# A two-layer graph attention kernel: fewer pairs in the edge count, and one weight load behind a row

## The chip, the cores and the metric

The kernel runs on one core of one Trainium2 chip. The metric is the device time in microseconds (us) of one launch, as the median of several runs; the kernel before takes 647.35 us (three runs, 647.07 to 647.61). In what follows PE is TensorE (matrix products), DVE is VectorE, ACT is ScalarE, POOL is GpSimd and SP is SyncE, which here only issues DMA transfers. Instructions of one engine start in program order; the engines meet at semaphores.

## The reference

The input is a graph of 512 nodes with 768 features each and 16,896 directed edges: 8,192 random pairs in both directions and 512 self loops, sorted by destination. Two graph attention layers follow each other, the first with 8 heads that are concatenated, the second with one; a residual sum and a layer norm close it.

```python
def gat_layer(x, W, a_s, a_d, b, edge_index, concat):
    h = (x @ W).reshape(n, H, C)
    alpha_s = jnp.einsum('nhc,hc->nh', h, a_s)
    alpha_d = jnp.einsum('nhc,hc->nh', h, a_d)
    e = jax.nn.leaky_relu(alpha_s[src] + alpha_d[dst], NEG_SLOPE)
    m = jax.ops.segment_max(e, dst, num_segments=n)
    e = jnp.exp(e - m[dst])
    denom = jax.ops.segment_sum(e, dst, num_segments=n)
    alpha = e / (denom[dst] + EPS)
    out = jax.ops.segment_sum(h[src] * alpha[:, :, None], dst, num_segments=n)
    ...
h = jax.nn.elu(gat_layer(x, W1, a_src1, a_dst1, b1, edge_index, concat=True))
out = gat_layer(h, W2, a_src2, a_dst2, b2, edge_index, concat=True)
return _layernorm(x + out)
```

Everything is float32.

## The kernel before

**Dense attention.** The kernel works with a 512 x 512 matrix `cnt` that holds how often each (destination, source) edge occurs, and `absent`, a large negative number where it doesn't occur. Per head, a 128-row block of scores is lifted from the row of source logits (`lift`, L465, ACT), bent (`leak`, L471, DVE), lowered to its maximum over the present edges (`rank`, L474, DVE, then an exponential on ACT), weighted with `cnt` and normalised (`weigh`, DVE), and transposed by a DMA (`turn_out` and `turn_in`) into `PT`.

**Products.** All large products are done in seven half-size products, P1 to P7, instead of eight. The sums that this needs of weights are made by loads that add on arrival (issued by POOL, L108 and L119) and by DVE (L303, L304); those of activations by DVE (L291 to L294, L744 to L758). Per head there are three stages: `projection` (x times W1 of the head: 14 products of three matmuls, L311), `mixed` (aggregation over the sources, L783, with the bias and ELU) and `second` (times the 768 rows of W2 that belong to the head, L311, added into `h2`). Each weight slot exists once: head h+2's W1 is loaded into the slots that head h+1's projection has read, and W2 alternates with it in another set.

**Counting the edges.** The first 62 us also make `cnt`. The destinations are sorted, so the 132 chunks of 128 consecutive edges each touch only a narrow span of destination nodes. Chunk c has its centre at m = (c + 0.5) * 128 * 512 / 16896. The kernel cuts the 512 destinations into 16 blocks of 32 and fixes, when it is built, which blocks each chunk may touch: the block of m, and a neighbour if m lies closer than `SLACK` nodes to that neighbour (L228 to L234). Each (chunk, block) is a pair; there are 210, and 78 of the chunks have two. For a pair, a 32-wide one-hot of the destinations (`od`, L509, DVE, a quarter of the chunks at a time, from `rel`, L265, the destination minus the first node of the block) is multiplied with a 512-wide one-hot of the chunk's sources (`os`, L532 on DVE or, for the blocks of the third 128-row block of `cnt`, a step function on ACT, L530). This is a matmul of 128x32 by 128x512 (L558). The result takes 32 rows of a 128-row PSUM bank; the pairs wait in four queues by their place among the four 32-row groups, and `count` (L547) takes one from each queue a round, so that four matmuls in different column groups of the array follow each other.

The order is written out by hand (L578 to L642): nine batches of 16 chunks (the last of 4). For each, DVE makes its one-hots; then a few products of head 0's first projection (`items`) and some DVE extras go out, with ACT making the step functions of the next batch between them; then `count` runs on what is queued. What doesn't fill a round stays queued for the next batch. 32 buffers hold the `os` one-hots; a new one-hot has to wait until the matmuls that read the old one are done.

`below`, `found` and `flag` (L514 to L520, L575) count the pairs whose destination lies in its block. If an edge falls into none of its chunk's blocks the whole pass is done again in a general way (L32); the block rule therefore decides speed, not the result.

**Head 0, and the queues around it.** SP's queue holds, in order: the four DMA transposes of head 0's weights of attention, `load_w2(0)` (L830: one 576 KB and six 384 KB transfers; POOL adds two more on arrival), then in the loop over heads `load_w1(h + 2)` (L854: again seven on SP and two adding ones on POOL), then `row_out` (L454), which is called from inside `mixed`: DVE transposes the source logits (L457), SP writes them in four small transfers to a scratch row in DRAM (L460) and reads them back spread over 128 partitions (L463). Behind it follow the next head's vectors (`load_a`, L868) and four loads for a logit product (`attended`, L841 to L844). `lift(h + 1, 0)` on ACT needs the row. In the loop, the order on DVE is written out too: P1 and P2 of `second` are emptied, the gT sums and two W2 sums are made, and only then `leak` and `rank` of the next head's scores follow.

Of the kernel before, what the change touches and what calls it, by code (L numbers as in the profile page):

```python
# [36 lines left out]
def gat_pass(  # L37
# [18 lines left out]
    N, D = x.shape  # L56
    H = a_src1.shape[0]
# [44 lines left out]
    def load_w(W, h, slot, m):  # L102


        t1 = wpool.tile([P, HK, HALF], F32, name=f"{slot}t1")
        upper = m[:HK * P, :].rearrange("(k p) d -> p k d", p=P)
        nc.sync.dma_start(t1, upper[:, :, L])
        nc.gpsimd.dma_start(t1, upper[:, :, R], accum_op=ALU.add)  # L108
        W[h] = []
        for r in range(2):  # L110
            w = wpool.tile([P, HK, D], F32, name=f"{slot}{r}")
            for k in range(r * HK, (r + 1) * HK):
                nc.sync.dma_start(w[:, k - r * HK, :], m[k * P:(k + 1) * P, :])
            W[h].append(w)
        W[h].append(t1)

        def rest():

            nc.gpsimd.dma_start(W[h][0][:, :, R], m[HK * P:, R].rearrange("(k p) d -> p k d", p=P),  # L119
                                accum_op=ALU.add)  # L120
        return rest

    def load_w1(h, slot="w2"):
        return load_w(W1, h, slot, w1[:, h * D:(h + 1) * D])
# [79 lines left out]
    def turn_x(t, r):  # L204

        ps = mm.tile([P, 512], F32, name="mm")
        for k in range(HK):
            nc.tensor.transpose(ps[:, k * P:(k + 1) * P], x_sb[:, t, (r * HK + k) * P:(r * HK + k + 1) * P], ident)
        nc.scalar.copy(xT[:, r * HK:(r + 1) * HK, t * P:(t + 1) * P],
                       ps[:, :HALF].rearrange("p (k n) -> p k n", n=P))  # L210
# [4 lines left out]
    if general:  # L215
        nc.vector.tensor_copy(idx_f, idx_i)
        idx = ohp.tile([P, 2, EC], F32, name="idx")
        psi = tr.tile([P, 512], F32, name="tr")
        for j in range(2):
            for r in range(2):  # L220
                nc.tensor.transpose(psi[:, (2 * j + r) * EH:(2 * j + r + 1) * EH], idx_f[:, j, r, :],
                                    ident[:EH, :EH])
        nc.vector.tensor_copy(idx, psi[:, :2 * EC].rearrange("p (j c) -> p j c", j=2))
    else:

        B, SLACK = 32, 10  # L228
        blocks = []
        for c in range(EC):  # L230
            m = (c + 0.5) * P * N / E
            b = int(m // B)
            lo, hi = b - (m - b * B < SLACK), b + ((b + 1) * B - m < SLACK)
            blocks.append(range(max(lo, 0), min(hi, N // B - 1) + 1))  # L234
        at = [0]
        for b in blocks:
            at.append(at[-1] + len(b))
        NB = at[EC]
        assert NB + EC <= 512 and max(map(len, blocks)) <= 2


        pick = ohp.tile([EH, NB], F32, name="pick")
        base = ohp.tile([P, NB], F32, name="base")
        lo = 0
        while lo < EC:
            hi, k = lo + 1, len(blocks[lo])
            while hi % EH and blocks[hi] == blocks[lo]:
                hi += 1
            copy = nc.vector.tensor_copy if lo < 5 * EC // 8 else nc.scalar.copy
            copy(pick[:, at[lo]:at[hi]].rearrange("p (c k) -> p c k", k=k),  # L250
                 ident[:EH, lo % EH:(hi - 1) % EH + 1].unsqueeze(2).to_broadcast([EH, hi - lo, k]))
            for j, b in enumerate(blocks[lo]):
                nc.gpsimd.memset(base[:, at[lo]:at[hi]].rearrange("p (c k) -> p c k", k=k)[:, :, j], float(b * B))
            lo = hi
        nc.vector.tensor_copy(idx_f, idx_i)
        turn_x(0, 0)
        psi = tr.tile([P, 512], F32, name="tr")
        for r in range(2):
            cols = slice(at[r * EH], at[(r + 1) * EH])
            nc.tensor.matmul(psi[:, cols], idx_f[:, 0, r, :], pick[:, cols], start=True, stop=True)  # L260
        for r in range(2):
            nc.tensor.transpose(psi[:, NB + r * EH:NB + (r + 1) * EH], idx_f[:, 1, r, :], ident[:EH, :EH])
        turn_x(1, 0)
        rel = ohp.tile([P, NB], F16, name="rel")
        nc.vector.tensor_tensor(rel, psi[:, :NB], base, op=ALU.subtract)  # L265
        idx = ohp.tile([P, EC], F32, name="idx")
        nc.vector.tensor_copy(idx, psi[:, NB:NB + EC])
# [582 lines left out]
                times(R, b1_[:, D:], -1.0, V2)]  # L850

    for h in range(H - 1):
        if h + 2 < H:
            load_w1(h + 2)()  # L854
        else:
            A[H] = []
            for j, a in ((2, a_src2[0]), (4, a_dst2[0])):
                v = wpool.tile([P, HK, HALF], F32, name=f"w2t{j}").rearrange("p k n -> p (k n)")[:, :D]
                nc.sync.dma_start(v, row_bcast(a))
                A[H].append(v)  # L860
            last_sum = load_w2(H - 1, "w2")
        GA, gsums = left(gT, gS)
        halves = [half_logits(h + 1, t) for t in ((0, 1) if h else (0, 1, 3))]
        besides[2:2] = [s_ for s_, _ in halves] + [lambda: row_out(h + 1)]
        finish = mixed(h, AA, BB, besides + [d_ for _, d_ in halves])
        besides = []
        if h + 2 < H:
            load_a(h + 2, a_src1[h + 2], a_dst1[h + 2])  # L868
            attend = attended(h)
        pairs = second(h, GA, B2)  # L870
        for m, _ in pairs[:2]:
            m()
        pairs[0][1]()
        for f in finish:
            f()
        gsums[0]()
        pairs[1][1]()
        gsums[1]()
        if pending:
            pending.pop(0)()  # L880
        pairs[2][0]()
        gsums[2]()
        pairs[3][0]()
        gsums[3]()
        if pending:
            pending.pop(0)()
        pairs[2][1]()
        pairs[3][1]()
        last = h + 2 == H
        q = [lift(h + 1, 0)]  # L890
        for n in range(2, 7):
            (m0, e0), (m1, e1) = pairs[2 * n:2 * n + 2]
            m0()
            if not last:
                m1()
            if n < 6:
                leak(q[n - 2])
                rank(q[n - 2], n - 2)
            if n < 5:
                q.append(lift(h + 1, n - 1))  # L900
            if last:

                if n > 4:
                    turn_in(n - 5)
                if n == 6:
                    turn(q[2], 2)
                if n == 6:
                    weigh(q[3], 3)
                m1(lambda: turn(q[3], 3) if n == 6 else None)
            if not last and n == 6:  # L910
                turn_in(0)
                weigh(q[2], 2)
                turn_out(q[2], 2)
            e0()
            if last and 2 < n < 6:
                weigh(q[n - 3], n - 3)
                if n < 5:
                    turn_out(q[n - 3], n - 3)
            if not last and 3 < n < 6:
                weigh(q[n - 4], n - 4)  # L920
                turn_out(q[n - 4], n - 4)
            if not last and n == 6:
                weigh(q[3], 3)
                turn_out(q[3], 3)
                load_w2(h + 1)()
            e1()
        if h + 2 < H:
            B_, sums = right(W1[h + 2], "w2")
            pairs = projection(h + 2, XA, B_)
            for n in range(14):  # L930
                pairs[n][0]()
                if n == 0:
                    for f in attend:
                        f()
                    B2, sums2 = right(W2[h + 1], "w1")
                if n in (1, 3):
                    sums[n // 2]()
                if n == 1:
                    AA, sums3 = left_sums(h + 1)
                pairs[n][1]()  # L940
                if n in (1, 2, 4):
                    turn_in((n + 2) // 2)
                if n == 5:
                    BB, sums3 = right_sums()
                if 1 <= n < 9:
                    sums3.pop(0)()
                if n in (9, 10):
                    sums2.pop(0)()
                if n in (11, 13):
                    logits(h + 2, HS[h + 2], 2 + (n - 11) // 2)  # L950
        else:
            last_sum()
            B2, sums2 = right(W2[H - 1], "w1")
# [162 lines left out]
```

## Time and profile before

| what | value |
| --- | --- |
| median of three runs | 647.35 us |
| the profiled execution, own time | 647.49 us |
| its span | 645.7 us |
| PE, busy share of the span | 98% |
| DVE | 80% |
| ACT | 44% |
| POOL | 7% |
| mean granted TensorE clock | 0.998 |
| DMA traffic | 100.32 MB, mean 155 GB/s |

The page gives busy time of each engine and the chain of work that ended last. A matmul of 128x384 in float32 shows up as two records of 487 ns that overlap, so a product of three matmuls (six records) takes 2.06 us of PE. Times of the timeline are microseconds from the start of the span; in its lines the figure after the start is how long the group took, the bracket is how long the engine was idle before it and what ended that.

### The profile page before, as it was taken

The page shows a single profiled execution, that of the slowest core. Times are in us where ns is not written, and L with a number is a line of the kernel's source. Part 1 is how long each engine was busy: PE and PEld are TensorE (multiplying, and loading weights), DVE is VectorE, ACT ScalarE, POOL GpSimd, SP SyncE. Part 2 cuts the span into 40 slices and gives each one's busy share as a digit, 9 for nine tenths or more (in the row PEclk, how much of TensorE's full clock was granted, in tenths as well). Part 3 has the DMA queues.
Part 4 walks back from the last instruction along what each step waited for, and adds up shares of the span by engine and source line. Part 5 has one row for each costly group of instructions (what it writes and reads, how often), then busy time and mean ns, then how long its engine had stood idle before and what let it go on. Part 6 is the DMA issues. An engine that isn't in the chain of part 4 may idle for free.

```text
span 645.7 us, 7216 instructions
## 1 busy us (share of the span) xinstructions
PE 634.5 (98%) x2347; PEld 400.6 (62%) x2347; DVE 519.7 (80%) x1149; ACT 281.8 (44%) x484; POOL 46.7 (7%) x90
## 2 busy tenths in 40 slices
PE   8999999999999999999999999999999999999995
PEld 5544585556855586556855586556855586645553
DVE  8999989978789677877789677877789677876885
ACT  6774744530725035430726035430726035543440
POOL 1310020011000110011000110011000110000000
PEclk9999999999999999999999999999999999999999
DMA  9993499296816793196816694196806890410122
GB/s 317 329 208 87 81 334 282 47 262 195 185 48 146 176 257 138 33 259 189 200 36 141 182 257 138 33 261 199 189 36 153 219 257 16 109 47 0 34 57 77
DMA packets 81017, 100.32 MB, mean 155 GB/s; under 512 B 39574, under 2 KB 62926, under 8 KB 80974
## 3 DMA queue, kind: packets, MB, share of 16 engines
q1 hardware_dynamic: 67310, 78.18, 39.2%
q0 software_dynamic: 12976, 20.65, 18.4%
q10 hardware_dynamic: 688, 0.98, 0.5%
q8 instruction: 20, 0.33, 0.2%
q14 instruction: 23, 0.19, 0.1%
HBM read 86.93 MB, written 1.59 MB: 137 GB/s over the span
## 4 chain that ended last, share of the span: by engine, by line
PE 93%; DVE 5%; ACT 0%; issue 0%; DVEq 0%
PE mm L311 62%; PE mm L783 20%; PE mm L729 3%; PE mm L1062 3%; PE held L311 2%; DVE os L532 1%; PE tr L558 1%; PE bc L181 1%; DVE odw L509 1%; DVE scr L320 0%; PE bc L558 0%; PE tr L986 0%; DVE h L367 0%; DVE q L477 0%; DVE q L472 0%
## 5 line engine op out<-in xcount | busy, mean ns | idle before, releaser
L311 PE MATMUL mm<-w,gT 128*128 128x384 f32 x288 | 96.8, 488 | 0.2 <-DVE u L367 0.2
L311 PE MATMUL mm<-w,xT 128*128 128x384 f32 x264 | 88.2, 487 | 0.0
L311 PEld LDWEIGHTS mm<-w,gT 128*128 128x128 f32 x288 | 54.3, 190 | 38.1 <-issue 1.6
L311 PEld LDWEIGHTS mm<-w,xT 128*128 128x128 f32 x264 | 49.9, 190 | 35.5 <-ACT os L530 0.8
L787 ACT COPY u<-mm 128x256 f32<-128x256 f32 x21 | 7.8, 372 | 140.5 <-PE mm L783 140.5
L479 ACT ACTIVATE q<-q,nmax 128x512 f32<-128x512 f32 x36 | 25.8, 721 | 89.5 <-DVE nmax L477 89.5
L783 PE MATMUL mm<-PT,hs 128*128 128x256 f32 x252 | 61.3, 379 | 0.0
L311 PE MATMUL mm<-w1t,gS 128*128 128x384 f32 x180 | 60.6, 486 | 0.0
L311 PE MATMUL mm<-w2t,xS 128*128 128x384 f32 x168 | 56.6, 487 | 0.0
L783 PEld LDWEIGHTS mm<-PT,hs 128*128 128x128 f32 x252 | 47.8, 190 | 8.3 <-issue 0.4
L369 DVE TENSOR_TENSOR h<-h,mm 128x384 f32<-128x384 f32 x72 | 39.1, 550 | 12.5 <-PE mm L311 12.0
L311 PEld LDWEIGHTS mm<-w1t,gS 128*128 128x128 f32 x180 | 34.1, 190 | 24.2 <-issue 0.6
L311 PEld LDWEIGHTS mm<-w2t,xS 128*128 128x128 f32 x168 | 31.8, 190 | 22.4 <-ACT q L468 0.4
L783 PE MATMUL mm<-pS,gS 128*128 128x256 f32 x168 | 43.2, 380 | 0.0
L711 ACT COPY PT<-zr 128x1024 uint16<-128x1024 uint16 x34 | 39.5, 1162 | 2.6 <-DMA zr<-pS 1.9
L783 PEld LDWEIGHTS mm<-pS,gS 128*128 128x128 f32 x168 | 31.8, 190 | 4.7 <-DVE pS L756 0.4
L706 ACT COPY pS<-q 128x1024 uint16<-128x1024 uint16 x26 | 27.2, 1045 | 16.6 <-DVE q L691 16.6
L311 PE MATMUL mm<-w1t,gT 128*128 128x384 f32 x96 | 32.4, 487 | 0.5 <-DVE h L367 0.5
L311 PE MATMUL mm<-w,gS 128*128 128x384 f32 x96 | 32.6, 486 | 0.0
L311 PE MATMUL mm<-w,xS 128*128 128x384 f32 x96 | 32.5, 487 | 0.0
L108 POOL DMA_DIRECT2D w1t<-in_L_gnn_W_dram x7 | 8.9, 1267 | 309.0 <-DVE w2t L304 142.3
L369 DVE TENSOR_TENSOR u<-u,mm 128x384 f32<-128x384 f32 x28 | 15.4, 553 | 18.8 <-PE mm L311 18.7
(190 smaller groups left out, 1083.9 us busy)
## 6 DMA issues: line engine op xcount, KB each, us to landing
w<-in_L_gnn_W_dram SPq DMA_DIRECT2D x90, 384.0 KB
w<-in_L_gnn_W_dram POOLq DMA_DIRECT2D x16, 576.0 KB, 9.0
w2t<-in_L_gnn_W_dram SPq DMA_DIRECT2D x10, 576.0 KB
w1t<-in_L_gnn_W_dram SPq DMA_DIRECT2D x9, 576.0 KB
w2t<-in_L_gnn_W_dram POOLq DMA_DIRECT2D x8, 576.0 KB, 9.2
w1t<-in_L_gnn_W_dram POOLq DMA_DIRECT2D x7, 576.0 KB, 8.7
a_s<-in_L_gnn_a_src_dram SPq DMA_DIRECT2D x8, 384.0 KB
a_d<-in_L_gnn_a_dst_dram SPq DMA_DIRECT2D x8, 384.0 KB
```

The costliest lines, as they stand in the source:

```text
L108: nc.gpsimd.dma_start(t1, upper[:, :, R], accum_op=ALU.add)
L181: nc.tensor.matmul(idle, zeros[:, :P], zeros, start=True, stop=True)
L311: nc.tensor.matmul(ps[:, :HALF], A_[p][:, k, i * P:(i + 1) * P], B_[p][:, k, :], start=start and k == 0, stop=k == HK - 1, skip_group_chec ...
L369: nc.vector.tensor_tensor(a, a, ps, op=ALU.subtract if p == "P7" else ALU.add)
L479: nc.scalar.activation(q, q, AF.Exp, bias=nmax, scale=-1.0)
L509: nc.vector.tensor_tensor(od[:, lo:hi, :], rel[:, lo:hi].unsqueeze(2).to_broadcast([P, hi - lo, B]), nodes[:, :B].unsqueeze(1).to_broadcas ...
L706: nc.scalar.copy(apart.rearrange("p (h n) -> p h n", h=2), q.bitcast(U16).rearrange("p (n h) -> p h n", h=2))
L711: nc.scalar.copy(PT.rearrange("p s n -> p (s n)").bitcast(U16).rearrange("p (s n h) -> p s n h", s=NT, h=2)[:, :, t * P:(t + 1) * P, :], p ...
L729: nc.tensor.matmul(ps[:, :N], HS[h][:, s, c * P:(c + 1) * P], PT[:, s, :], start=(s == 0), stop=(s == NT - 1))
L783: nc.tensor.matmul(bank[p][:, :HN], A_[p][:, k, c * P:(c + 1) * P], B_[p][:, k, :], start=over is None and k == 0, stop=k == 1, skip_group ...
L787: nc.scalar.copy(u, part("P1"))
L1062: nc.tensor.matmul(ps[:, :cols.stop - cols.start], PT[:, s, t * P:(t + 1) * P], h2[:, s, cols], start=(s == 2), stop=(s == 1))
```

## The change

Two things change. The slack that decides which blocks a chunk is paired with is no longer 10 nodes everywhere, but 2 + 16 * sqrt(p * (1 - p)) with p = m / 512, the chunk's place in the sorted list: 3.0 at the ends, 8.9 at a quarter, 10 in the middle. That gives 196 pairs in place of 210, and 64 chunks with two blocks in place of 78. And in head 0 (h = 0 of the loop) `load_w1(2)` is called after `mixed`, hence behind `row_out` on SP, and ahead of `load_a`; in the other heads it stays where it was.

```diff
-        B, SLACK = 32, 10
+        B = 32
         blocks = []
         for c in range(EC):
             m = (c + 0.5) * P * N / E
             b = int(m // B)
-            lo, hi = b - (m - b * B < SLACK), b + ((b + 1) * B - m < SLACK)
+            slack = 2 + 16 * (m / N * (1 - m / N)) ** 0.5
+            lo, hi = b - (m - b * B < slack), b + ((b + 1) * B - m < slack)
             blocks.append(range(max(lo, 0), min(hi, N // B - 1) + 1))
...
     for h in range(H - 1):
-        if h + 2 < H:
+        if 0 < h < H - 2:
             load_w1(h + 2)()
-        else:
+        elif h:
             A[H] = []
...
         finish = mixed(h, AA, BB, besides + [d_ for _, d_ in halves])
         besides = []
+        if h == 0:
+            load_w1(2)()
         if h + 2 < H:
             load_a(h + 2, a_src1[h + 2], a_dst1[h + 2])
             attend = attended(h)
```

## The prediction

> **What bounds the kernel now.** I read the table of busy time first, then the chain that ended last, then busy time by stretch, then the timeline of the two places that the diff touches.
>
> The page and the stretches (cut at the joints of the chain) give the room:
>
> ```profile
> PE 634.5 (98%) x2347; PEld 400.6 (62%) x2347; DVE 519.7 (80%) x1149; ACT 281.8 (44%) x484; POOL 46.7 (7%) x90
> ...
> core 0: us, PE busy (x) PEld busy (x) DVE busy (x) ACT busy (x) POOL busy (x), PEclk, DMA share, GB/s
> 0.00:20.72 20.72, 18.73 (x112) 10.20 (x112) 17.61 (x67) 14.52 (x36) 3.50 (x56) 1.00 0.94 333
> 20.72:41.79 21.07, 20.77 (x122) 10.76 (x122) 19.52 (x50) 14.76 (x28) 5.92 (x5) 1.00 1.09 279
> 41.79:61.80 20.01, 19.14 (x131) 9.47 (x131) 19.10 (x58) 10.99 (x21) 1.78 (x2) 1.00 0.54 116
> 61.80:100.42 38.62, 38.59 (x145) 27.13 (x145) 34.42 (x82) 24.37 (x42) 4.68 (x4) 1.00 0.75 203
> 100.42:117.55 17.13, 16.42 (x50) 8.69 (x48) 16.29 (x29) 5.41 (x10) 0.41 (x1) 1.00 0.82 223
> 117.55:637.50 519.95, 519.92 (x1784) 333.58 (x1785) 410.35 (x859) 210.74 (x350) 30.42 (x24) 1.00 0.54 140
> ```
>
> PE is the bound, and from 117.55 on without a gap. Before that it idles 1.99 + 0.30 + 0.87 + 0.03 + 0.71 us. So a change gains by fewer PE instructions or out of these gaps. The chain shows what closes each gap:
>
> ```profile
> 19.80 0.88 DVE xS L291
> 20.72 6.07 PE mm L311 x18
> ...
> 40.93 0.19 DVE os L532
> 41.19 0.56 DVE hs L434
> 41.79 4.14 PE held L311 x12
> ...
> 58.77 0.60 ACT steps L409
> 59.47 0.69 DVE cnt L411
> 60.16 1.06 DVE os L532 x4
> ...
> 112.86 0.61 DVE q L472
> 113.49 0.69 DVE q L477
> ```
>
> Three joints of the count are on DVE: the sum xS at 20.72, the adds of L434 at 41.79, and at the end `cnt` with the last four one-hots. In head 0 it is DVE again, which empties P7 late (117.55).
>
> **Part 1, the pairs.** Fourteen pairs go: 14 matmuls of L558 and 14 x 32 = 448 elements of `od`. The queue rule of `count`, applied to both lists, gives the rounds per batch: 6, 6, 7, 7, 5, 9, 7, 6, 4 before (57), and 5, 6, 6, 7, 4, 9, 6, 5, 4 after (52). A round costs 0.217 us: batch 5, 9 rounds, runs from 45.86 to 47.92 (2.06); batch 7, 6 rounds, from 57.67 to 59.08 (1.41); the difference over three rounds. One DVE one-hot goes (batch 4: 13 to 12) and one ACT step (batch 6: 5 to 4). What of this lies on the path:
>
> - *Up to 20.72* DVE runs without a pause from `rel` at 6.41. `od` of 1728 elements took 1.95 us and of 1632 1.85, so 1.04 ns an element; the first quarter falls from 1632 to 1440 (0.20), the third from 1728 to 1696 (0.03); `rel` and the two instructions of `below` lose 14 elements of 210 each (about 0.04 together, from 0.38, 0.22 and 0.38 us). xS comes 0.27 earlier, and PE with it: it idled 0.28 there. Batch 0's saved round is covered by this same wait: 0.
> - *Batch 2*, 26.91 to 28.54: PE has no gap around it, one round less is 0.22 at once.
> - *Batch 4 and 41.79.* At 40.66 DVE waited for the first matmuls of this batch to free `os` buffers, and then made two one-hots ahead of the L434 add that PE needs. With a one-hot less in batch 4 the rotation shifts by one, and only one is made after that wait: 0.27 (16 one-hots took 4.28). The saved round doesn't count, since PE waits for the add anyway. That leaves the second `od` of 1440 (0.20) and the missing one-hot ahead of 40.66: hidden by the wait.
> - *Batches 6 and 7.* Batch 6 loses a round, 0.22. From 41.19 to 59.11 DVE is busy throughout with the same list after as before, and idles 0.35 ahead of `cnt`. The third block of `cnt` is complete in the fourth round of batch 7 in both lists, so batch 7's saved round doesn't bring it forward; `cnt` starts 0.97 earlier where DVE could have started 0.76 + 0.35 = 1.11 earlier. Batch 8 then paces by its four one-hots: unchanged, four rounds.
>
> The pick copies and POOL's memsets keep their number (32 and 48), only sizes change: 0. Sum: 0.27 + 0.22 + 0.27 + 0.22 = 0.98 us. Bounds: no less than the two rounds in gapless places, 0.43; at most all five rounds and the start, 5 x 0.217 + 0.27 = 1.36. I take 0.98, because at each joint the timeline names the wait. After 61.80 all work up to 82 hangs on this end (lifts, transposes, right sums) and shifts with it.
>
> **Part 2, the load behind the row.** Nine DMAs move: seven on SP pass behind the row's five, two on POOL (576 KB each, adding) start later; POOL's next is at 137.57, so it isn't held.
>
> ```profile
> 95.90 1.49 SPq L460 DMA_DIRECT2D drow<-turned  x4
> 105.37 0.35 SPq L463 DMA_DIRECT2D q<-drow  x1
> 109.20 0.72 ACT L468 ACTIVATE q<-q,al_d 128x512 f32<-128x512 f32 x1 [5.86 <-DMA q<-drow]
> 111.84 1.02 DVE L367 TENSOR_SCALAR h<-mm 128x384 f32<-128x384 f32 x2
> 112.78 0.68 DVE L472 SCALAR_TENSOR_TENSOR q<-q 128x512 f32<-128x512 f32 x1
> 129.26 7.90 PE L311 MATMUL mm<-w,xT 128*128 128x384 f32 x24
> ```
>
> The four small writes wait 7.4 us in head 0 and 2.1 and 3.0 in the next two heads, so the row will land some 5 us earlier, and the lift can start when the destination logits are done, at 103.9. What waited for the lift? ACT only. DVE starts the leak at 112.78, without idling, after the L367 copies that stand ahead of it; it has run back to back since 100.62, longer than the lift's late end (109.92). The second lift stands behind an exponential that needs that leak. So nothing on DVE or PE moves: gain 0. Upper bound: all of the 0.71 us that PE idles here.
>
> The cost: SP now waits for `turned` (95.88) and the row before W1(2), about 99.5 to 100.4 by the other heads' waits, where it issued from 81.74. Behind it lie 576 + 6 x 384 KB, two adding loads of 576, the next vectors (2 x 384) and `attended` (1152): 6.1 MB. From 78 to 113.5 the same queue moved 10.5 MB, 296 GB/s; so 20.6 us, done at 120 to 121. First need: PE at 129.26 for W1's first blocks (they go first and are in by 107), DVE at 130.07 for `attended`, 132.15 for the block with the first adding load, PE at 140.87 for the other. Nine us of slack, and SP's next transposes (123.02) find the queue empty: 0.
>
> **Sum.** 647.49 - 0.98 = 646.5 against the profiled execution. That stands 0.14 above the median of the three runs, so the median should come to 646.4, 0.15% less.
>
> **Rivals.**
> *Faster by more than 0.2% (1.3 us; about what a measurement of this kernel can tell from no change).* Either all five rounds count (1.36, 646.0), for which speaks that PE is 96% busy in the count, against it the three DVE joints; or the early row does loosen head 0 (0.98 + 0.71 = 1.69, 645.7), against which stands that DVE's order is the same and that no DVE wait there names the row.
> *Slower: the weights come late.* If W1(2)'s first adding load lands after 135.6 (132.15 plus the 3.5 us from the end of L303 to P6 at 137.00), each us holds PE for one; slower by 1.3 needs 2.3 us more, landing at 137.9 or later; one us beyond that is 649.7. A rule speaks for it. Row: POOL's issue of an adding load took 1.26 to 1.28 us between 82 and 100, but 1.99 at 31.37, beside DVE's one-hots. The Trainium skill, SBUF — State Buffer, section "Who interferes with whom", says that some VectorE modes (copy, cast, tensor_scalar) lock GpSimd out of a shared port for the whole instruction, which starves descriptors of loads issued by POOL. By that rule at its worst both loads would wait for DVE's first pause, 115.1: with the longest landing of the stretch, 12.2 us, that is 127.3, and no time is lost; the trace shows such a delay (0.7 us) beside one-hots alone. The slack shrinks, so I give this rival some chance, not much.
> *The change does nothing*, 647.0 to 647.4: if the DVE chain held the whole count. Against it: PE gaps are only 0.30 and 0.87 us in those 41 us. A second pass (`again`), some 650 us more, would need an edge outside its blocks; the drawn list strays at most 4.9 nodes from m, and none lies outside.
>
> **How the numbers follow.** Forecast, 0.43 to 1.29 us gained (646.06 to 646.9): 0.47. Faster than that: 0.36, mostly just beyond the line. Nothing gained, within 0.2%: 0.05. Slower by over 0.2%: 0.12. So faster 0.36, same 0.52, slower 0.12. The predicted time is 646.4. The range reaches up to the case without gain, 647.4, and down to 1.69 us and the runs' spread of 0.3 below it, 645.4; it leaves out the slower rival and little else. The likeliest case alone has 646.06 to 646.9.
>
> **What the profile after would show.** L558 with 196 matmuls; `od` of 1440 and 1696 elements; PE at 61.80 resuming near 60.8, with xS near 20.45 and L434's add near 40.4. L463 issued near 99, ACT's 5.86 us wait gone, but the leak still directly behind L367 and the gap ahead of P4 (0.50) unchanged. I am wrong if 61.80 moves by less than 0.4 or more than 1.3 us, if the stretch from there to 117.55 changes its length by over 0.2 us, or if PE shows a wait on a weight near 128 to 141.

## The result, and the profile after

The changed kernel takes 646.67 us (median of 22 runs, 646.20 to 647.37), the kernel before 647.43 us (22 runs, 647.07 to 648.07). The ratio is 0.9986 with a 95% interval of 0.998 to 0.9992: 0.76 us less, or with the interval 0.5 to 1.3 us. That is a gain, and a smaller one than 0.2%; 646.4 was forecast.

The first part of the page of the changed kernel:

```profile
PE 633.4 (98%) x2333; PEld 399.9 (62%) x2333; DVE 518.2 (80%) x1148; ACT 281.4 (44%) x483; POOL 47.7 (7%) x90
```

Fourteen matmuls, one DVE instruction and one ACT instruction fewer, as counted. Busy time by stretch, cut at the same joints as before (sum xS ready, add of `hs` ready, first product after the count, P4 of head 0):

```profile
core 0: us, PE busy (x) PEld busy (x) DVE busy (x) ACT busy (x) POOL busy (x), PEclk, DMA share, GB/s
0.00:20.64 20.64, 18.24 (x109) 9.96 (x109) 17.29 (x67) 14.31 (x35) 3.46 (x56) 1.00 0.93 328
20.64:41.23 20.59, 20.34 (x116) 10.55 (x116) 18.50 (x49) 15.34 (x29) 6.96 (x5) 1.00 1.08 282
41.23:61.03 19.80, 19.03 (x127) 9.27 (x127) 19.10 (x58) 10.26 (x20) 1.77 (x2) 1.00 0.58 121
61.03:116.76 55.73, 55.00 (x194) 35.82 (x193) 50.67 (x111) 29.65 (x51) 5.09 (x4) 1.00 0.73 200
116.76:636.70 519.94, 519.91 (x1784) 333.58 (x1785) 410.19 (x859) 210.80 (x350) 30.42 (x24) 1.00 0.55 142
```

Read the first column of figures against the stretches before. The second is 0.48 us shorter (21.07 before), the third 0.21 (20.01), and from 61.03 on nothing has changed: 55.73 us for 55.75, 519.94 for 519.95. So all that was won up to 636.70 was won in the count. (The last 8 us, which the change doesn't touch, took 8.2 in the execution before and 7.9 in this one; from P4 to the end it is 527.7 to 528.2 us in the ten kernels here that have no long pause on PE, whatever the kernel.) The first stretch looks only 0.08 shorter, but it doesn't begin at the same point in the two executions: the first cast of the edge list on DVE, which waits for the list to land, starts at 5.01 before and at 5.21 after. From that cast to the joint it is 15.71 before and 15.43 after. The DVE chain that leads to xS begins with `rel`, and here are its first instructions, before and after:

```profile
6.41 0.38 DVE L265 TENSOR_TENSOR rel<-tr,base 128x210 f16<-128x210 f32 x1 [0.98 <-PE tr L262]
...
6.98 1.79 DVE L509 TENSOR_TENSOR odw<-rel,nodes 128x1632 bf16<-128x1632 f16 x1
```

```profile
6.60 0.36 DVE L266 TENSOR_TENSOR rel<-tr,base 128x196 f16<-128x196 f32 x1 [0.97 <-PE tr L263]
...
7.16 1.59 DVE L510 TENSOR_TENSOR odw<-rel,nodes 128x1440 bf16<-128x1440 f16 x1
```

From `rel` on DVE has no pause up to xS, and the product that uses xS starts 14.31 us behind `rel` before and 14.04 after.

The chain of waits of the changed kernel, at the DVE steps of the three joints (start, duration, what):

```profile
19.73 0.87 DVE xS L292
...
40.37 0.03 DVE os L533
...
40.63 0.56 DVE hs L435
...
58.69 0.69 DVE cnt L412
59.38 1.06 DVE os L533 x4
```

The same three releasers as before, each earlier. What DVE makes between its wait for a buffer and the add of `hs`, before and after:

```profile
40.66 0.62 DVE L532 TENSOR_SCALAR os<-nodes,idx 128x512 bf16<-128x512 f16 x2 [0.73 <-PE tr L558]
```

```profile
40.36 0.35 DVE L533 TENSOR_SCALAR os<-nodes,idx 128x512 bf16<-128x512 f16 x1 [0.93 <-PE tr L559]
```

One one-hot stands there in place of two. Head 0 in the timeline of the changed kernel (start, duration, engine and line, what, idle time before it):

```profile
95.12 1.29 SPq L461 DMA_DIRECT2D drow<-turned  x4
97.41 0.35 SPq L464 DMA_DIRECT2D q<-drow  x1
...
102.46 0.71 ACT L469 ACTIVATE q<-q,al_d 128x512 f32<-128x512 f32 x1
...
111.06 1.01 DVE L368 TENSOR_SCALAR h<-mm 128x384 f32<-128x384 f32 x2
111.99 0.68 DVE L473 SCALAR_TENSOR_TENSOR q<-q 128x512 f32<-128x512 f32 x1
...
116.76 4.14 PE L312 MATMUL mm<-w1t,gT 128*128 128x384 f32 x12 [0.49 <-DVE h L368]
```

The row is read back at 97.41, where it was 105.37; the lift on ACT follows at 102.46 with no wait for a DMA. But the leak on DVE still stands directly behind the copies of L368, and PE still waits 0.49 us for the next of these copies. An earlier row moved nothing that counts.

### The profile page after: what moved, and what is told of

It is laid out like the page before. It is cut to its first block, busy times and chain, and to the rows that moved or that the text cites. A ratio compares the mean times of both kernels' runs of the same rounds, so it can differ in the third digit from the quotient of the medians.

```text
span 644.6 us, 7189 instructions
## 1 busy us (share of the span) xinstructions
PE 633.4 (98%) x2333; PEld 399.9 (62%) x2333; DVE 518.2 (80%) x1148; ACT 281.4 (44%) x483; POOL 47.7 (7%) x90
## 4 chain that ended last, share of the span: by engine, by line
PE 93%; DVE 5%; DMA 1%; issue 0%; ACT 0%; SPq 0%; DVEq 0%
PE mm L312 62%; PE mm L784 20%; PE mm L730 3%; PE mm L1065 3%; PE held L312 2%; DVE os L533 1%; PE tr L559 1%; DMA idx_i<-in_src_dram 1%; DVE scr L321 0%; PE bc L559 0%; PE tr L989 0%; DVE odw L510 0%; DVE h L368 0%; DVE q L478 0%; DVE q L473 0%
## 5 line engine op out<-in xcount | busy, mean ns | idle before, releaser
L784 PE MATMUL mm<-PT,hs 128*128 128x256 f32 x252 | 61.3, 379 | 0.0
L784 PEld LDWEIGHTS mm<-PT,hs 128*128 128x128 f32 x252 | 47.8, 190 | 8.3 <-issue 0.4
L784 PE MATMUL mm<-pS,gS 128*128 128x256 f32 x168 | 43.2, 380 | 0.0
L784 PEld LDWEIGHTS mm<-pS,gS 128*128 128x128 f32 x168 | 31.8, 190 | 4.7 <-DVE pS L757 0.4
```

What stands on the lines that cost most here:

```text
L784: nc.tensor.matmul(bank[p][:, :HN], A_[p][:, k, c * P:(c + 1) * P], B_[p][:, k, :], start=over is None and k == 0, stop=k == 1, skip_group ...
```

## The experiments

The joints of the count repeat to 0.01 us from execution to execution once they are taken from one PE instruction to the next, while the start of the first product after xS scatters with what lands when (20.31 to 21.70 us over the kernels below, of which their own edits make at most 0.6). So each kernel is read by its stretches. This table has them in us. Its first column goes from `rel` on DVE to the first product with xS, and repeats to 0.01 us too wherever that product follows the end of xS; the others go from joint to joint in the timeline of PE: the first product with xS (20.72 before), the first of `held` behind the add (41.79), the first product after the count (61.80), and P4 (117.55).

| kernel | rel to xS's product | xS to held | held to end of count | end of count to P4 |
| --- | --- | --- | --- | --- |
| before | 14.31 | 21.07 | 20.01 | 55.75 |
| changed | 14.04 | 20.59 | 19.80 | 55.73 |
| pairs only | 14.05 | 20.59 | 19.79 | 55.73 |
| row only | 14.32 | 21.07 | 20.00 | 55.72 |
| pairs, chunks of the first half | 14.47, PE late | 20.85 | 20.00 | 55.73 |
| pairs, chunks of the second half | 15.32, PE late | 20.80 | 19.79 | 55.72 |
| changed, W1(2) behind `attended` | 14.05 | 20.59 | 19.79 | 55.71 |
| changed, P7's copy first | 14.04 | 20.60 | 19.79 | 55.06 |
| 180 pairs | 13.75 | 19.84 | 19.15 | 55.73 |
| 180 pairs, P7's copy first | 13.75 | 19.84 | 19.14 | 55.07 |

### The pairs alone

The changed kernel, with the load put back where it was:

```diff
-        if 0 < h < H - 2:
+        if h + 2 < H:
             load_w1(h + 2)()
-        elif h:
+        else:
...
-        if h == 0:
-            load_w1(2)()
```

> Part 1 alone: the kernel before with the 196 pairs, W1(2) still ahead of the row. My theory: all of the gain is here, 0.98 us or 0.15% (ratio 0.9985), as in the whole change; in the profile P4 of head 0's second product still starts about 0.5 us after PE could. If the row loosened head 0, this kernel would gain less than the whole change, by up to 0.7 us (ratio 0.9996 to 0.9985).

Measured: 646.76 us (11 runs), ratio 0.9984 [0.9975, 0.9993]. The stretches are those of the changed kernel to 0.01 us. The whole gain lies in the pairs.

### The row alone

The kernel before, with nothing but the moved load (the reverse of the edit above):

> Part 2 alone: 210 pairs, W1(2) behind the row. My theory: the row is read back some 8 us earlier (97 to 98 in place of 105.4), ACT's wait of 5.9 us is gone, and the time stays (ratio 0.9998 to 1.0002): the leak still starts directly behind the copies of P2 near 112.8. If the row were what holds head 0: 0.3 to 0.7 us less (ratio 0.999 to 0.9995). If the weights came late: slower, with a PE wait between 129 and 141.

Measured: 647.44 us (11 runs), ratio 0.9999 [0.999, 1.0008], and stretches as before. Its timeline:

```profile
98.34 0.35 SPq L463 DMA_DIRECT2D q<-drow  x1
...
112.92 0.68 DVE L472 SCALAR_TENSOR_TENSOR q<-q 128x512 f32<-128x512 f32 x1
...
117.69 1.56 PE L311 MATMUL mm<-w1t,gT 128*128 128x384 f32 x4 [0.50 <-DVE h L367]
```

The row is read back 7 us earlier than in the kernel before, the leak comes 0.14 later and P4 0.14 later, which is no more than the later start of this execution (cast at 5.18, against 5.01). The row was off the path.

### Each half of the pairs

The new slack for half of the 132 chunks, the old one for the others; the load where it was. One profiled execution of each.

```diff
-            slack = 2 + 16 * (m / N * (1 - m / N)) ** 0.5
+            slack = 2 + 16 * (m / N * (1 - m / N)) ** 0.5 if c < EC // 2 else 10
```

> The kernel before, with the new slack for the first 66 chunks alone: 203 pairs, a round less in batch 0 and in batch 2, no one-hot less. Times are taken from the first cast of indices on (5.01 in the kernel before), so that the landing of the index list doesn't enter. My theory: xS 0.25 earlier (20.72), after batch 2 0.47 (28.54), and this 0.47 stays at 41.79 and at the end of the count (61.80). If each round counted: 0.43 plus 0.25, 0.68 at the end. If the end were held by DVE alone: 0.25 or less.

> The kernel before, with the new slack for the last 66 chunks alone: 203 pairs, a round less in batches 4, 6 and 7, a one-hot less in batch 4. My theory, from the first cast on: 0.04 at xS, 0.04 after batch 2, then a step of 0.27 at 41.79 (the one-hot, not the round), a step of 0.22 at 53.61 (batch 6), nothing more: 0.53 at the end. If rounds counted and one-hots didn't: steps of 0.22 at 41.79, 53.61 and 59: 0.69 at the end.

Measured: 646.96 us for the first half and 647.58 us for the second, one execution each, against 647.78 us (median of nine) of the kernel before. These single times scatter by as much as what is asked, so the timelines decide. First half, second half:

```profile
20.50 1.56 PE L312 MATMUL mm<-w1t,xS 128*128 128x384 f32 x4
...
41.35 1.88 PE L312 MATMUL held<-w1t,xT 128*128 128x384 f32 x5 [0.30 <-DVE hs L435]
...
61.35 1.88 PE L312 MATMUL mm<-w2t,xS 128*128 128x384 f32 x5
```

```profile
21.70 0.59 PE L312 MATMUL mm<-w1t,xS 128*128 128x384 f32 x1
...
42.50 0.91 PE L312 MATMUL held<-w1t,xT 128*128 128x384 f32 x2 [0.25 <-DVE hs L435]
...
62.29 0.91 PE L312 MATMUL mm<-w2t,xS 128*128 128x384 f32 x2
```

Between the joints on PE the first half wins 21.07 - 20.85 = 0.22 us and then 0.01: the round of batch 2 and nothing else. The second half wins 21.07 - 20.80 = 0.27 (the one-hot ahead of the add, in batch 4) and 20.01 - 19.79 = 0.22 (the round of batch 6). These are three of the four terms of the forecast, each by itself. The fourth, the start, shows in these two executions on DVE alone: from `rel` to the end of xS it takes 14.05 us in the first half and 14.21 in the second, where the kernel before has 14.26, so 0.21 and 0.05 less. PE didn't profit, since it came to its product later than xS: it had waited 0.29 us for its first weights of x times W1 in the one, and 0.34 and 0.54 in the other, whose start at 21.70 is therefore not its edit. So the forecasts from the cast to the end of the count (0.47 and 0.53 earlier) were missed by these two executions as a whole, 0.08 earlier and 0.51 later, while their steps behind xS came as forecast.

### The row made late

In the kernel before, SP is made to issue the loads of the logit product ahead of `row_out`, twice over; the second set has to wait for the slots of the first. Four loads more are moved than the kernel needs.

```diff
             load_w1(h + 2)()
+        if h == 0:
+            attended(0)
+            attend = attended(0)
+        if h + 2 < H:
+            pass
         else:
...
-            attend = attended(h)
+            if h:
+                attend = attended(h)
```

> The kernel before, with the four loads for the logit product of head 0 put ahead of the row and issued twice, so that the row lands late. Estimate from the queue's 296 GB/s: row read back at 115 to 118 in place of 109.2. My theory: the row has 2.9 us of slack (lift ends 109.9, leak starts 112.8), and what is beyond it costs PE one for one: 4 to 7 us slower (ratio 1.006 to 1.011). If scores were hidden however late: ratio 1.000.

Measured: 659.49 us (4 runs), ratio 1.0186 [1.0171, 1.0202], about 12 us more. The timeline of SP, DVE and PE:

```profile
97.39 0.33 SPq L844 DMA_DIRECT2D w2t<-in_L_gnn_a_dst_dram  x1
112.20 0.33 SPq L841 DMA_DIRECT2D w2t<-in_L_gnn_W_dram  x1
...
114.00 1.36 SPq L460 DMA_DIRECT2D drow<-turned  x4
118.72 0.36 SPq L463 DMA_DIRECT2D q<-drow  x1
...
122.86 0.69 DVE L472 SCALAR_TENSOR_TENSOR q<-q 128x512 f32<-128x512 f32 x1 [10.04 <-ACT q L468]
...
127.64 5.98 PE L311 MATMUL mm<-w1t,gT 128*128 128x384 f32 x12 [10.63 <-DVE h L367]
133.45 4.03 PE L311 MATMUL mm<-w1t,gS 128*128 128x384 f32 x12
```

The 4 to 7 us that were expected are missed, because the edit delayed the row by far more than was estimated: SP stood from 97.4 to 112.2 until the first set had landed, and the lift that waits for the row started at 122.1, where the row had been estimated for 115 to 118. What follows from the delay is as expected: the leak comes 10.1 us late (112.78 before), so does P4 (117.55 before), one for one. The row can be late up to the time at which DVE is through with the copies of L367, and no longer. That accounts for 10.1 of the 12 us. The rest is in the block behind the pause: its twelve records take 5.98 us where they took 4.14 before. Busy time by stretch shows why, in the column PEclk:

```profile
core 0: us, PE busy (x) PEld busy (x) DVE busy (x) ACT busy (x) POOL busy (x), PEclk, DMA share, GB/s
116.00:121.00 5.00, 1.01 (x4) 0.26 (x2) 0.00 (x0) 0.00 (x0) 0.00 (x0) 1.00 0.40 112
121.00:127.60 6.60, 0.00 (x0) 0.00 (x0) 4.20 (x10) 2.51 (x4) 0.00 (x0) 0.51 0.34 125
127.60:131.30 3.70, 3.66 (x6) 2.15 (x7) 1.84 (x4) 2.21 (x4) 0.00 (x0) 0.50 0.00 0
131.30:140.00 8.70, 8.70 (x28) 5.08 (x28) 7.93 (x23) 4.08 (x6) 0.00 (x0) 1.00 0.17 31
```

PE's last record ends at 117.0; from 121.1 its granted clock is 0.50, and it is full again only at 131.4, 3.7 us after PE resumed. From the start of P4 to the next product it is 5.81 us, against 3.97 before: 1.84 us. With the 10.09 of the pause that makes 11.9.

### How much slack the weights have

The moved load is put further back in head 0, in two steps: behind `attended`, and behind the transposes of the next head's scores. The edit of the first step (in the second, the two added lines stand behind `turn_out(q[3], 3)`, ahead of `load_w2(h + 1)`):

```diff
-        if h == 0:
-            load_w1(2)()
         if h + 2 < H:
             load_a(h + 2, a_src1[h + 2], a_dst1[h + 2])
             attend = attended(h)
+        if h == 0:
+            load_w1(2)()
```

> The changed kernel, with W1(2) put back by six more loads (the next head's vectors and the four loads of the logit product, 1.9 MB): issued near 106 to 109 in place of 97.9. My theory: last transfers land at 121 to 125, first blocks by 115; still before the needs at 129 to 141, so the time is that of the changed kernel (ratio 0.9986 within 0.0006). If the slack were gone, PE would wait on a weight near 128 and the time would rise by more than 1 us.

Measured: 646.64 us (8 runs), ratio to before 0.9982 [0.9971, 0.9994]: the changed kernel's time. The last adding load is issued 11 us later than in the changed kernel (106.48 there):

```profile
117.57 1.27 POOL L119 DMA_DIRECT2D w<-in_L_gnn_W_dram  x1 [1.78 <-DMA w<-in_L_gnn_W_dram]
```

and no product waits for a weight.

> The changed kernel, with W1(2) put back as far as behind the four transposes of head 0's scores: issued near 130. My theory of what decides: first blocks land about 5 us after issue where PE wants them at 128.3, the adding loads about 10 to 15 us after issue; PE waits 6 to 12 us in sum: ratio 1.008 to 1.017. If the loads of weights had slack beyond what the needs show, less than 2 us.

Measured: 662.13 us, ratio 1.0221 [1.0189, 1.0254], 14.4 us above the kernel before: more than expected. W1(2) is issued from 131.6 on. What PE waited for, from 62 to 200 us (in all, times, longest), and the late block in the timeline:

```profile
PE mm L312 <- DMA w<-in_L_gnn_W_dram: 8.5, 2, 8.3
PE mm L312 <- DVE w2t L304: 2.4, 1, 2.4
```

```profile
137.19 10.83 PE L312 MATMUL mm<-w,xT 128*128 128x384 f32 x24 [8.29 <-DMA w<-in_L_gnn_W_dram]
```

Waits for weights make 10.9 us, and the block behind the pause took 10.83 us where the same 24 records take 7.90 in the changed kernel: 2.9 us more, again at a granted clock of 0.50, from 132.7 to 142.9. Together that is 13.8 us; where the next aggregation (L784) begins, this execution lies 14.5 us further behind its P4 than the changed kernel, and the remaining 0.7 us, most of it in the block behind the second wait, is not traced here. So between 11 us later (nothing lost) and some 34 us later (the wait in the open) lies the end of the slack; the rival "the weights come late" is a real mechanism, and the change stayed clear of it.

### The copy that PE waits for, ahead of the second leak

The profiles before and after name what holds P4: the next copy of L368, which on DVE stands behind the second leak and its maximum. Here, in head 0, this emptying (`e0`) is called ahead of them; otherwise it is the changed kernel.

```diff
+            early = h == 0 and n == 3
+            if early:
+                e0()
             if n < 6:
                 leak(q[n - 2])
                 rank(q[n - 2], n - 2)
...
-            e0()
+            if not early:
+                e0()
```

> The changed kernel, and in head 0 the emptying of P7's first half is put ahead of the second leak and rank on DVE. My theory: head 0's gap of 0.5 us is DVE's order and not a late row; the emptying fits into the 0.47 us that DVE idles there for the second lift, so P4 starts 0.5 us earlier: 0.5 us less than the changed kernel (ratio to the kernel before 0.9978). If the gap came from transfers, nothing changes against the changed kernel (0.9986).

Measured: 645.97 us (8 runs), ratio 0.9975 [0.9965, 0.9986], 0.8 us below the pairs alone on the same chip (646.76). DVE, and then PE:

```profile
114.70 0.56 DVE L368 TENSOR_SCALAR h<-mm 128x384 f32<-128x384 f32 x1
115.17 0.68 DVE L473 SCALAR_TENSOR_TENSOR q<-q 128x512 f32<-128x512 f32 x1
...
116.43 2.74 PE L312 MATMUL mm<-w1t,gT 128*128 128x384 f32 x8
```

The copy runs in the half microsecond in which DVE had waited for ACT, and P4 starts without a wait; the stretch falls from 55.73 to 55.06, 0.67 us where 0.5 was expected. This gap was open all along. It was the order on DVE that held it, not the row.

### Still fewer pairs

The slack narrowed to 2 + 10 * sqrt(p * (1 - p)): 180 pairs, 47 rounds. Edges of other lists would fall outside the narrower blocks sooner, and then the whole pass runs again; for this input none does.

```diff
-            slack = 2 + 16 * (m / N * (1 - m / N)) ** 0.5
+            slack = 2 + 10 * (m / N * (1 - m / N)) ** 0.5
```

> The changed kernel with the double counting distance at 10 in place of 16 (180 pairs counted, 16 fewer than in the changed kernel, with the list of this input still inside the pairs that are counted). Theory (the stretch up to 62 us is a chain that goes through TensorE and, where VectorE's emptyings end last, through VectorE): the joints come 0.46 us earlier after the start than in the kernel before, another 0.43 by the end of batch 2, 0.22 in batch 3, about 0.5 less at the held add, and at most 0.35 more at the count, because some of the rounds taken out lie beside VectorE's work: about 2.0 us less than before, 645.4, ratio 0.997. Rival (every round is TensorE's own time): ten rounds at 0.217 us and the shorter start 0.46 make 2.6 us, 644.8, ratio 0.996. Rival (VectorE bounds the stretch by now): no more than the changed kernel's gain, 646.6, ratio 0.9986.

> The same 180 pairs, and with it the order of e5_empty_first: in head 0 the emptying that the next stage waits for stands ahead of the second leak and its ranks on VectorE. Theory: the two gains lie one behind the other on the path (the first before 62 us, the second, 0.5 us, at 116 to 118 us), so they add: about 2.5 us less than before, 644.9, ratio 0.996. Rival (they overlap): the gain of the kernel with 180 pairs alone, ratio 0.997.

Measured: 645.10 us (5 runs), ratio 0.9963 [0.995, 0.9977], and with the copy first 644.09 us (5 runs), 0.9947 [0.9933, 0.9961]. The first lies between the theory (2.0 us) and its rival (2.6), and the interval holds both; the timeline says which terms were off:

```profile
6.86 0.34 DVE L266 TENSOR_TENSOR rel<-tr,base 128x180 f16<-128x180 f32 x1 [1.65 <-PE tr L263]
...
19.62 0.94 DVE L292 TENSOR_TENSOR xS<-xT 128x768 f32<-128x768 f32 x1
20.61 1.56 PE L312 MATMUL mm<-w1t,xS 128*128 128x384 f32 x4
...
39.30 1.02 DVE L435 TENSOR_TENSOR hs<-hs,held 128x384 f32<-128x384 f32 x2
40.45 2.85 PE L312 MATMUL held<-w1t,xT 128*128 128x384 f32 x8
...
58.49 1.18 PE L559 MATMUL tr<-os,odw 128*32 128x512 bf16 x7 [0.64 <-DVE os L533]
59.60 3.82 PE L312 MATMUL mm<-w2t,xS 128*128 128x384 f32 x11
```

PE shows no wait at 40.45 any more: the first of the two adds of L435, which PE needs, is done 0.6 us before, so this joint on DVE no longer binds, and a round is PE's own time. At 20.61 PE shows no wait either, but there the product still follows the end of xS (20.56) by 0.05 us, as it does in every kernel here in which PE is not the later one. The stretch up to `held` wins 1.23 us (the theory had 0.43 + 0.22 + 0.5), the next one 0.86 where the theory allowed 0.35: the wait at the end of the count stayed at 0.64, but all of it came earlier with the rounds. On the other side the start, for which 0.46 had been counted, gave 0.11 in this execution. The pairs are not the reason: from `rel` to the product it is 13.75 us, 0.56 less than before. But `rel` itself waited 1.65 us for PE's transposes of the edge list, against 0.98 before. Sum 2.2, measured 2.3. The two gains add, as expected: end of count to P4 is 55.07 with the copy first, 55.73 without, and the times differ by 1.01 us, of which 0.66 is this stretch; the 0.3 us by which that execution also started sooner are scatter (`rel` waited 0.96 us in it). This last kernel is the fastest of all, 0.5% below the kernel before.

## Why the prediction was right

- *The start, 0.27.* Held. Where the sum xS comes last, PE starts its product 15.71 us after the first cast with the old pairs (the kernel before; the row alone agrees: 5.18 to 20.90) and 15.43 after it with the new (the changed kernel, the copy first, the load behind `attended`): 0.28. From `rel` on it is 0.27 in each of the five kernels with the 196 pairs (14.04 to 14.05, against 14.31 to 14.32 in the three with 210: the kernel before, the row alone, the late row). Ahead of `rel` it can be lost: with the pairs alone the product came 15.65 after the cast, because `rel` waited 1.17 us for PE's transposes and not 0.97; and where first weights were late PE was the last to arrive. This term is the one that a single span can't show.
- *Batch 2, 0.22; the one-hot ahead of the add, 0.27; batch 6, 0.22.* Held, each shown alone by the two halves: 0.22, 0.27 and 0.22. The reason for the second is also as put: one `os` in place of two between the wait for a buffer and the add.
- *The rounds said to be hidden.* Held: batches 0, 4 and 7 add nothing. The start is shorter by DVE's 0.27 alone; the step at `held` is the one-hot's 0.27 and not a round's 0.22, and PE waits for that add before and after (0.30 and 0.25 us). In batch 7, counted from `held`, PE is through with it 0.43 us earlier, two rounds (16.86 for 17.29), and at the end of the count only one of them is left.
- *The row, 0.* Held. It was read back 8 us earlier, and the row alone has a ratio of 0.9999. The late row shows the other side: the slack ends where DVE finishes the copies of L367, and beyond it a microsecond costs a microsecond.
- *The weights, 0.* Held. Traffic stops between 119 and 121 us (the last adding load, issued at 106.48, lands 14.0 us later), for which 120 to 121 was forecast; no product waits. POOL's two issues took 1.26 and 1.27 us, so the delay behind DVE that the prediction weighed didn't come. A load issued some 11 us later still cost nothing. A detail was off: the four writes of the row waited 0.9 us and not 2.1 to 3.0, so that the read of the row went out at 97.4 and not near 99.
- *The sum.* 0.28 + 0.48 + 0.21 = 0.97 from the joints, 0.98 forecast. The medians differ by 0.76, with an interval that holds 0.97; with the pairs only it is 0.84, with W1(2) behind `attended` 1.14 below the kernel before on the same chip. Whether on average a part of the start's 0.28 is lost when other things come late is left open by these runs; it would be of the size of the difference between 0.76 and 0.97. The medians alone can't tell 0.97 from the 0.69 of the two stretches; the joints can.
- *The rivals.* "All five rounds count" fell with the stretches, for this size of the change; with 180 pairs it becomes nearly true, because the joint on DVE at the add of `hs` moves out of the way. "The early row loosens head 0" fell with the row alone. "The weights come late" exists, but from a point that lies beyond the moved load by more than 11 us.
- *Readings that were off, without a consequence.* The longest landing of an adding load in the stretch was 14.9 us (issued at 85.90) and not 12.2, which still leaves the worst case of that rule at 130.0, ahead of 135.6. The 10.5 MB between 78 and 113.5 are all of the core's traffic, POOL's loads with it, and not SP's queue alone. PE is 95% busy in the count by the stretches shown, not 96%. And DVE, said to be busy throughout from 41.19 to 59.11, waits 0.10 us for ACT at 51.32, and as long in the changed kernel. A product of three matmuls takes 1.94 us of PE where products follow each other (twelve records from 121.52 to 125.39), not the 2.06 said ahead of the prediction; no term rests on it.

## What to carry to other kernels

Work that is taken out of a stretch counts at the joints: ask at each wait of the bounding engine which of two chains ends last, and price the removed instruction only in the chain that does; and once several are gone, ask again, since the answer changes (180 pairs gave more for a round than 196 did). An earlier DMA is worth nothing while its consumer on the path stands behind other work in its own queue: look at what is ahead of the consumer, and reorder that. To see tenths of a microsecond, compare stretches between two fixed instructions of the same chain, not spans.

## What the runs showed of the hardware

A pause of PE costs more than its length. In the kernel with the late row the granted clock fell to 0.50 some 4.1 us after the last matmul and came back 3.7 us after the first; in the one with W1(2) behind the transposes it fell 3.8 us after the last and came back 5.7 us after the first (137.19 to 142.9), and the blocks behind the pauses took 1.8 and 2.9 us more. The Trainium skill, TensorE: Matmul & The Clock Gate, section "Part 1: The HAM clock gate", has the array at half clock after at least one idle window of about 3.4 us, and at full clock again after at least one busy one, in windows that run freely. These runs agree: the clock is halved, and all four times are longer than one such window, the longest being 5.7 us. A shorter pause, of 2.4 us, in the kernel with W1(2) behind the transposes (up to 150.41) left the clock at 1.00, and so did the waits of 0.5 and 0.2 us that this kernel normally has on PE after 62 us.

The beginning of the program scatters by more than the change is worth. The cast behind the landing of the edge list started between 4.64 and 5.55 us in these profiles, the nine first matmuls on zeros took from 3.57 to 4.02 us, and in one execution PE waited 0.9 us for its first weights. In three (pairs only, W1(2) behind the transposes, 180 pairs) `rel` waited 1.17 to 1.65 us for PE's transposes, in the other nine 0.96 to 0.98; in these three the transposes of x ahead of them (L208, three records) took 0.85 to 0.88 us, against 0.49 in the kernel before. The first product behind xS starts anywhere from 20.31 to 21.70.

POOL's issue of the adding loads beside a sum and one-hots of DVE, at 30.5 and 31.3 us, took 2.49 and 3.04 us in the profile of the changed kernel, against 1.44 and 1.99 before, with the same work around them. That is not the change: the row alone, with the old pairs, has 2.49 and 3.04 too, and W1(2) behind `attended`, with the new, 1.32 and 1.87. Why it varies, these runs don't show. Beside DVE's sums at 103.6 and 106.5 it took 1.26 and 1.27. No time hung on it here.
